# A new order inside the steps of layer 0: features first, the output product in the middle, routing last, the maxima unpromoted

## The chip, the cores and the metric

The kernel runs on one core of a Trainium2 chip. The metric is the device time of one execution in microseconds; three executions of the kernel before took 2866.75, 2875.81 and 2886.9 us, median 2875.81. The profile is of one further execution.

## The reference

A network of two layers works on 64 sequences of 128 rows and 128 features, with 77 context rows for each sequence. Each layer adds a gated attention to the context and then a gated mixture of 8 experts:

```
x = x + tanh(g_xattn[0]) * L0_attention(ctx, ctx, layernorm(x))
x = x + tanh(g_ffn[0])   * L0_experts(layernorm(x))
x = x + tanh(g_xattn[1]) * L1_attention(layernorm(x), ctx, ctx)
x = x + tanh(g_ffn[1])   * L1_experts(layernorm(x))
```

The change is in layer 0. Its attention has 16 heads. Queries, keys and values each go through the feature map `z = x @ fm_w.T + fm_b`, `[exp(z), exp(-z)]`, which makes 16 features of 8; scores are products of these over sqrt(128), softmax over the 77 context rows, a weighted sum of the value features, and an output product with `fc_w`. Its experts compute `silu(g) * u` on 336 inner features each and a down product; a router's softmax gives each expert's score, and a small second network picks for every row how many of the best experts count.

## The kernel before, in words

**Units and groups.** Layer 0's attention works on units of two sequences (32 units); the experts work on groups of four sequences (16 groups), so a group is two units. One unit passes through four generators, each in another step of the main loop in `run`:

- `l0_features` (step k for unit k): loads x and the context, layernorm on DVE and POOL, transposes into `pt`, the feature product `pz`, exponentials on ACT, transposes of the value features (`pv`), the split of the features into three bf16 parts (`split3`, DVE and POOL), the DMAs of these to DRAM (`dq`, `dk`) and back, stacked, into `qst` and `kst` (L331, L333).
- `l0_maxima` (step k+1): 32 products of `qst` and `kst` into the PSUM tile `S` (L346), six at a time, each group reduced to row maxima on DVE (L349); then the maxima are transposed (`pn`, L354), split in three on ACT, DVE and POOL (L357 to L360), and sent by three small DMAs into rows 96 to 98 of `qst` (L362).
- `l0_weighted` (step k+2): the transposed products, with the maxima subtracted inside the product (`ST`, L387), exponential on ACT (L390), the product with the value features (`AV`, L376), and at the end `od`, a DMA to DRAM, with `normalize`: DMAs, a reciprocal, and a POOL product that makes `o` (L437).
- `l0_project` (step k+3): the output product `pf` of `o` and `fc_w` (8 matmuls, L411) and the residual sum into `x1` (L413).

Every second step, from step 4 on, also holds `route` of the group whose second unit has just been projected: layernorm, transposes `ptf` (L449), the router's product `pr`, the small network, transposes into `pl` (L469, L470, L474), softmax and ranks on DVE, a split, and transposes `pp` (L590).

**The tape.** The experts' work is one long generator, cut into 33 parts a group. `tape(n)` plays n parts of it inside a step. A part is a hidden product (three matmuls each for `pg` and `pu`, L156 to L158, then ACT, DVE, DVE, ACT, POOL) or a down product (`py`), which begins with the expert's scores spread over a tile (`pb`, L599). `step` is given a target of `PARTS0 / 2 * (k + 1 - 5.0)` parts for step k, and plays as many as are missing.

**What sets the order.** `weave` interleaves a step's generators: each has a start and an end as shares of the step, its parts stand evenly between, and the parts are written into the program in the order of these positions. That is the program order. Each engine's list is planned from it before the run, on a modelled time line: of the instructions that are ready in the model, the one earliest in program order is taken. `high_priority(offset)`, the third number of an entry of `PLAN`, counts a part's instructions as if they stood that many places earlier. On the chip each engine works through its list in order and waits on semaphores where the data isn't there.

**Shared buffers.** Tiles of one tag take turns in program order. `pt`, `pz`, `pv`, `pn`, `pf`, `pl`, `pp` and `pb` all have the tag `misc` with one PSUM bank; `S`, `ST`, `AV` and `py` have one bank each; `pg`, `pu`, `ptf` and `pr` share three. `qst` has three buffers, `kst` three fixed tiles taken in turn.

**Queues.** SP issues all DMAs of layer 0, in one planned list.

After the last unit comes a transition: a step with the projection of unit 31, routing of group 15 and the first work of layer 1, planned with the same entries `out` and `rt0`; the later steps are layer 1's.

Of the kernel before, what the change touches and what calls it, by code (L numbers as in the profile page):

```python
# [41 lines left out]
def weave(tc, streams):  # L42


    todo = []
    for n, (gen, parts, lo, hi, pri) in enumerate(streams):
        todo.append([lo, n, gen, (hi - lo) / max(parts, 1), pri])
    while todo:
        t = min(todo, key=lambda x: (x[0], x[1]))
        try:  # L50
            if t[4]:
                with tc.high_priority(offset=t[4]):
                    next(t[2])
            else:
                next(t[2])
            t[0] += t[3]
        except StopIteration:
            todo.remove(t)


PARTS0, PARTS1 = 33, 24

PLAN = dict(
    out=(0, 0.2, 2000),
    wei=(0, 0.7, 0),
    max=(0.2, 0.95, 1000),
    fea=(0.2, 0.6, 1000),
    out1=(0.25, 0.4, 600),
    att1=(0.1, 0.95, 0),
    rel1=(0.37, 0.93, 0),  # L70
# [3 lines left out]
    t0=(0, 1.1, 0),  # L74
# [3 lines left out]
    prjT=(0, 0.55, 1000),  # L78
    attL=(0.1, 0.4, 500),
    prjL=(0.2, 0.3, 500),  # L80
    rt0=(0.1, 1, 500),
    rt1=(0.45, 0.7, 1000),
)

# [11 lines left out]
class Net:  # L96
# [947 lines left out]
    def run(self, ngroups):  # L1044
        tc, nc = self.tc, self.nc
        ctx = ExitStack()
        self.xs, self.routed = {}, {}
        self.done = 0
        self.ng = ngroups
        self.work = self.experts(ngroups)  # L1050

        self.fp = ctx.enter_context(tc.tile_pool(name="work", bufs=1))

        self.s3, self.ns3 = [], 0
        for n in range(2):
            t = self.fp.tile([128, GT], BF16, name=f"s3{n}", tag=f"s3{n}")
            nc.gpsimd.memset(t, 0.0)
            self.s3.append(t)
        ps = {n: ctx.enter_context(tc.tile_pool(name="ps" + n, bufs=1, space=PSUM)) for n in ("m", "S", "T", "A", "y")}
        self.pmisc, self.pS, self.pST, self.pY = ps["m"], ps["S"], ps["T"], ps["y"]  # L1060
        self.avp = ps["A"].tile([128, 4, 128], F32, tag="AV", name="AV")
        nc.vector.memset(self.avp, 0.0)
        gcm, self.pGU = self.pool("psg0", space=PSUM)
        self.gub = 3
        fcm, f0 = self.pool("f0")
        self.f0 = f0
        self.f0_open, self.ctx1 = (fcm, gcm), ctx
        acm, self.ap = self.pool("a0", side="right")
        self.l0_setup(f0, self.ap)
        nun = ngroups * 2  # L1070
        st = {}
        for k in range(nun + 2):
            w = []
            if 0 <= k - 3:
                w.append((self.l0_project(k - 3, st.pop(k - 3), self.xs), 1, *PLAN["out"]))
            if 0 <= k - 2 < nun:
                w.append((self.l0_weighted(st[k - 2]), 9, *PLAN["wei"]))
            if 0 <= k - 1 < nun:
                w.append((self.l0_maxima(st[k - 1]), 7, *PLAN["max"]))
            if k < nun:  # L1080
                w.append((self.l0_features(k, st), 5, *PLAN["fea"]))
            if k >= 4 and k % 2 == 0:
                w.append((self.route((k - 4) // 2), 6, *PLAN["rt0"]))
            self.step(w, 20, PLAN["t0"], math.ceil(PARTS0 / 2 * (k + 1 - 5.0)),
                      (k - 3) // 2 if k > 2 and k % 2 else None)
            if k == 1:
                with tc.issue_after(self.last_dma.ins):
                    self.l0_ffn_setup(f0)
        acm.__exit__(None, None, None)

        w1cm, w1 = self.pool("w1", side="right")
        self.l1_setup(w1)
        rpcm, self.rp = self.pool("rp", side="right")
        self.rqb, self.early = 2, 0
        acm, self.ap = self.pool("a1h", side="right")
        self.pp = self.ap
        self.l1_buffers(2)
        self.weights(2)
        self.banks = itertools.cycle(((self.pS, "S"), (self.pST, "ST")))
        s1 = {}  # L1100
        h0, h1 = (0, 0, 2), (0, 2, 2)
        self.step([(self.l0_project(nun - 1, st.pop(nun - 1), self.xs), 1, *PLAN["out"]),
                   (self.route(ngroups - 1), 6, *PLAN["rt0"]),
                   (self.l1_project(*h0, s1), 8, *PLAN["prjT"]),
                   (self.l1_relate(h0, s1), 7, *PLAN["relT"])], 27, PLAN["t0"])
        self.step([(self.l1_attend(s1[h0], 2), 13, *PLAN["attL"]),
                   (self.l1_project(*h1, s1), 8, *PLAN["prjL"]),
                   (self.l1_relate(h1, s1), 7, *PLAN["relL"])], self.parts(ngroups) - self.done, PLAN["t0"])
        while self.f0_open:
            next(self.work)  # L1110
        for k in range(1, ngroups + 3):
            w = []
            u = (k - 2, 0, 4) if k > 2 else h1 if k == 2 else h0
            if k == 2:
                weave(tc, [(self.l1_out(*u, s1.pop(u)), 3, 0, 1, 600), (self.tape(6), 6, 0, 1, 0)])
            elif k - 2 < ngroups:
                w.append((self.l1_out(*u, s1.pop(u)), 3, *PLAN["out1"]))
            if k == 2:

                acm.__exit__(None, None, None)  # L1120
                rpcm.__exit__(None, None, None)
                rpcm, self.rp = self.pool("rp4", side="right")
                self.rqb, self.early = 3, 2
                acm, self.ap = self.pool("a1", side="right")
                self.weights(4)
            if k == 1:
                w.append((self.l1_attend(s1[h1], 2), 13, *PLAN["attL"]))
            elif k - 1 < ngroups:
                w.append((self.l1_attend(s1[k - 1, 0, 4], 4), 23, *PLAN["att1" if k < ngroups else "attE"]))
            if k < ngroups:  # L1130
                w.append((self.l1_project(k, 0, 4, s1), 8, *PLAN["prj1"]))
                w.append((self.l1_relate((k, 0, 4), s1), 13, *PLAN["rel1"]))
            if 0 <= k - 2 < ngroups:
                w.append((self.route(ngroups + k - 2), 6, *PLAN["rt1"]))
            self.step(w, 28, PLAN["t1" if k < ngroups else "tE"],
                      self.parts(ngroups) + PARTS1 * (k + 1 - 3.0), ngroups + k - 2 if k > 2 and k - 2 < ngroups else None)
        for _ in self.tape(1000):
            pass
        for cm in (acm, rpcm, w1cm, self.ppcm):
            cm.__exit__(None, None, None)  # L1140
        ctx.close()
# [105 lines left out]
```

## Time and profile before

| | |
|---|---|
| median of three runs | 2875.81 us |
| profiled execution | 2871.89 us |
| its span, first to last instruction | 2870.2 us |
| mean granted TensorE clock | 0.921 |
| layer 0, first feature product to last projection | 6.1 to 1395.2 us |
| PE, DVE, ACT, POOL busy, 130 to 1330 us | 1053.29, 936.19, 674.30, 662.67 of 1200 us |
| PE busy, 0 to 130 us | 66.13 us |
| DMA queue of SP (q1), whole span | 246.28 MB, 42.8% of the time of 16 engines |

How to read it: busy time is per engine, PEld is the weight load that runs beside PE's matmuls, and PEclk is the clock granted to TensorE in tenths. A line of waits names the engine, the tile and line that waited, what came last before it could go on, the total in microseconds, how often, and the longest. In a timeline row stand the start, the duration, the engine, the line, the operation and its tiles (output, arrow, inputs), and in brackets the idle time of the engine before it with what ended it. Layer 0 is best read in its steady part, 130 to 1330 us; before that its pipeline fills, after it the two layers overlap.

### The profile page before, as it was taken

The numbers are of one execution on the slowest core, as the hardware profiler recorded it, in microseconds if no ns is written. First come the engines' busy times: TensorE is split into PE (matmuls) and PEld (weight loads), VectorE is DVE, ScalarE is ACT, GpSimd is POOL, SyncE is SP. The second block draws the span as 40 slices with busy tenths as digits, with TensorE's granted clock in tenths as the row PEclk, the third lists the DMA queues.
The fourth block names the chain that finished last, engine by engine and source line by source line (L and its number), as shares of the span: only waits on it lengthen the run. The fifth ranks groups of instructions, "written<-read, shape, count | busy, mean of one in ns | idle before, by whom it ended". The sixth has DMA issues, their size and how long they took to land.

```text
span 2870.2 us, 61032 instructions
## 1 busy us (share of the span) xinstructions
PE 2452.1 (85%) x23631; PEld 1668.7 (58%) x23638; DVE 1935.3 (67%) x4054; ACT 1579.2 (55%) x3030; POOL 1574.0 (55%) x1508
## 2 busy tenths in 40 slices
PE   3788898888888888988887878898988889889887
PEld 2455665666566565656554556566665666556654
DVE  3468787777878778777764555566566666656655
ACT  2455565555555555555543445566655556556556
POOL 4455555565545555455645535565555556555556
PEclk9989999999999999999986778899999999999998
DMA  6743534544445445343244655554554556555500
GB/s 144 163 103 96 106 91 83 116 98 95 97 84 105 107 93 101 87 85 77 77 84 108 137 104 119 116 110 108 109 115 104 118 119 126 116 105 113 108 16 8
DMA packets 504412, 290.56 MB, mean 101 GB/s; under 512 B 264614, under 2 KB 480814, under 8 KB 504027
## 3 DMA queue, kind: packets, MB, share of 16 engines
q1 hardware_dynamic: 476475, 246.28, 42.8%
q10 hardware_dynamic: 27648, 40.38, 4.0%
q8 instruction: 186, 3.05, 0.4%
q14 instruction: 103, 0.84, 0.1%
HBM read 147.19 MB, written 138.60 MB: 100 GB/s over the span
## 4 chain that ended last, share of the span: by engine, by line
PE 42%; DVE 19%; DMA 18%; POOL 8%; issue 7%; ACT 4%; SPq 3%; ACTq 0%; POOLq 0%; DVEq 0%
PE py L156 3%; PE ST L827 3%; PE py L157 3%; DMA qst<-dq 2%; DMA qst<-n 2%; PE py L158 2%; PE AV L376 2%; PE pz L156 2%; DVE t L508 2%; PE pg L156 2%; POOL hl L987 2%; PE S L770 2%; DVE t L509 2%; DMA kst<-dk 2%; PE ST L387 2%
## 5 line engine op out<-in xcount | busy, mean ns | idle before, releaser
L515 POOL TENSOR_TENSOR hl<-t,hh 128x512 fp32r<-128x512 f32 x336 | 454.0, 1357 | 345.3 <-ACT hh L514 339.0
L987 POOL TENSOR_TENSOR hl<-t,hh 128x512 fp32r<-128x512 f32 x256 | 345.2, 1362 | 111.6 <-ACT hh L986 111.1
L819 POOL TENSOR_TENSOR sc<-sc,mx 128x308 f32<-128x308 f32 x256 | 192.1, 752 | 216.0 <-DVE mx L818 139.5
L507 ACT ACTIVATE t<-pg 128x512 f32<-128x512 f32 x336 | 200.7, 598 | 160.6 <-PE pg L158 104.3
L514 ACT CAST hh<-t 128x512 fp32r<-128x512 f32 x336 | 207.8, 619 | 137.4 <-DVE t L509 58.0
L613 DVE TENSOR_TENSOR ys<-sb,py 128x512 f32<-128x512 f32 x224 | 153.2, 684 | 190.0 <-ACT sb L604 105.0
L828 ACT ACTIVATE rel<-ST 77x512 f32<-77x512 f32 x256 | 157.9, 617 | 187.3 <-PE ST L827 185.7
L508 DVE SCALAR_TENSOR_TENSOR t<-t,pg 128x512 f32<-128x512 f32 x336 | 226.8, 675 | 40.7 <-ACT t L507 40.2
L509 DVE TENSOR_TENSOR t<-t,pu 128x512 f32<-128x512 f32 x336 | 226.7, 675 | 10.8 <-PE pu L158 3.8
L604 ACT COPY sb<-pb 128x512 f32<-128x512 f32 x256 | 150.3, 587 | 134.7 <-PE pb L599 88.5
L817 DVE TENSOR_TENSOR sc<-S,rq 128x308 f32<-128x308 f32 x256 | 121.4, 475 | 147.8 <-PE ST L827 73.2
L986 ACT CAST hh<-t 128x512 fp32r<-128x512 f32 x256 | 158.5, 624 | 109.8 <-PE py L158 82.7
L614 POOL TENSOR_TENSOR acc<-acc,ys 128x512 f32<-128x512 f32 x96 | 133.6, 1391 | 154.5 <-DVE ys L613 154.2
L390 ACT ACTIVATE P<-ST 77x512 f32<-77x512 f32 x256 | 151.1, 591 | 120.3 <-PE ST L387 115.5
L979 ACT ACTIVATE t<-pz 128x512 f32<-128x512 f32 x256 | 153.3, 599 | 71.6 <-POOL hl L987 64.3
L827 PE MATMUL ST<-ident,sc 128*128 128x128 f32 (+1 forms) x1024 | 182.8, 307 | 5.1 <-ACT sg L776 1.6
L349 DVE TENSOR_REDUCE mx<-S 128x5 f32<-128x385 f32 (+1 forms) x192 | 110.3, 576 | 107.4 <-PE S L346 106.5
L156 PE MATMUL pu<-xh,wu_h 128*128 128x512 f32 x336 | 159.1, 473 | 21.9 <-DVE t L508 20.7
L156 PE MATMUL pg<-xh,wg_h 128*128 128x512 f32 x336 | 161.4, 480 | 15.7 <-DVE t L509 10.2
L157 PE MATMUL py<-hl,wd_h 128*128 128x512 f32 x336 | 150.9, 449 | 23.3 <-POOL hl L515 22.8
L156 PE MATMUL py<-hh,wd_h 128*128 128x512 f32 x336 | 152.0, 452 | 17.8 <-DVE ys L613 13.4
L827 PEld LDWEIGHTS ST<-ident,sc 128*128 128x128 f32 (+1 forms) x1024 | 131.7, 157 | 43.3 <-issue 14.2
(248 smaller groups left out, 6572.1 us busy)
## 6 DMA issues: line engine op xcount, KB each, us to landing
rq<-ra SPq DMA_DIRECT2D x256, 154.0 KB
qst<-dq SPq DMA_DIRECT2D x96, 384.0 KB
ra<-sg ACTq DMA_DIRECT2D x128, 192.5 KB
kst<-dk SPq DMA_DIRECT2D x96, 231.0 KB
dq<-f SPq DMA_DIRECT2D x47, 384.0 KB
od<-av SPq DMA_DIRECT2D x32, 512.0 KB
ra<-sg ACTq DMA_DIRECT2D x64, 231.0 KB
dq<-f SPq DMA_DIRECT2D x47, 256.0 KB
```

Source lines behind the costliest of these rows:

```text
L156: nc.tensor.matmul(ps, lhsT=wh, rhs=xh, start=start, stop=False)
L157: nc.tensor.matmul(ps, lhsT=wh, rhs=xl, start=False, stop=False)
L507: nc.scalar.activation(t, pg, AF.Tanh, scale=0.5)
L508: nc.vector.scalar_tensor_tensor(t, t, 1.0, pg, ALU.add, ALU.mult)
L509: nc.vector.tensor_tensor(t, t, pu, ALU.mult)
L514: nc.scalar.copy(hh, t)
L515: nc.gpsimd.tensor_tensor(hl, t, hh.bitcast(F32), ALU.subtract)
L819: nc.gpsimd.tensor_tensor(sc, sc, m.unsqueeze(2).to_broadcast([128, 4, KL]), ALU.subtract)
L827: nc.tensor.transpose(st[:r, j, :], sc.rearrange("q j k -> q (j k)")[:, j * KL : j * KL + r], self.ident)
L828: nc.scalar.activation(relg[:KL, hg, b], st[:KL].rearrange("k j (q e) -> k j q e", e=2), AF.Exp, scale=1.0 / math.sqrt(HD))
L986: nc.scalar.copy(hh, t)
L987: nc.gpsimd.tensor_tensor(hl, t, hh.bitcast(F32), ALU.subtract)
```

## The change

Only the positions, the promotions and one constant of layer 0's steps change:

- features: from 0.2 to 0.6 of a step to 0 to 0.4, still 1000 places ahead;
- the output product of the unit of three steps ago: from the start of the step (2000 places ahead) to 0.5 (1000 ahead);
- routing: from 0.1 to 1 to 0.55 to 1, still 500 ahead;
- the maxima: from 0.2 to 0.95 with 1000 places ahead to 0.1 to 0.85 with none;
- the weighted products: from 0 to 0.7 to 0.1 to 0.75, with no promotion before or after;
- the experts' target: 5.3 steps behind instead of 5.0;
- the transition's step gets entries of its own (`outT`, `rtT`) with the old values.

No instruction is added or taken out.

```diff
 PLAN = dict(
-    out=(0, 0.2, 2000),
-    wei=(0, 0.7, 0),
-    max=(0.2, 0.95, 1000),
-    fea=(0.2, 0.6, 1000),
+    out=(0.5, 0.55, 1000),
+    outT=(0, 0.2, 2000),
+    rtT=(0.1, 1, 500),
+    wei=(0.1, 0.75, 0),
+    max=(0.1, 0.85, 0),
+    fea=(0, 0.4, 1000),
...
-    rt0=(0.1, 1, 500),
+    rt0=(0.55, 1, 500),
...
-            self.step(w, 20, PLAN["t0"], math.ceil(PARTS0 / 2 * (k + 1 - 5.0)),
+            self.step(w, 20, PLAN["t0"], math.ceil(PARTS0 / 2 * (k + 1 - 5.3)),
...
-        self.step([(self.l0_project(nun - 1, st.pop(nun - 1), self.xs), 1, *PLAN["out"]),
-                   (self.route(ngroups - 1), 6, *PLAN["rt0"]),
+        self.step([(self.l0_project(nun - 1, st.pop(nun - 1), self.xs), 1, *PLAN["outT"]),
+                   (self.route(ngroups - 1), 6, *PLAN["rtT"]),
```

## The prediction

> **What bounds the kernel now.** I read the page first, then the windows by stage, then PE's waits in the longest stage of layer 0, then stretches of the timeline. The page names PE:
>
> ```profile
> PE 2452.1 (85%) x23631; PEld 1668.7 (58%) x23638; DVE 1935.3 (67%) x4054; ACT 1579.2 (55%) x3030; POOL 1574.0 (55%) x1508
> PEclk9989999999999999999986778899999999999998
> ```
>
> The change touches layer 0, so the stage that counts is its steady part, 130 to 1330 us. There PE works 1053.29 of 1200 us and DVE 936.19 (78%):
>
> ```profile
> 130.00:1330.00 1200.00, 1053.29 (x7111) 717.12 (x7104) 936.19 (x1829) 674.30 (x1317) 662.67 (x569) 0.95 0.45 97
> ```
>
> So 147 us of PE's time are idle, and this is what they waited for:
>
> ```profile
> PE S L346 <- DMA kst<-dk: 55.0, 24, 4.8
> PE pu L156 <- DVE t L508: 19.3, 31, 1.5
> PE py L157 <- POOL hl L515: 17.2, 15, 2.3
> PE py L156 <- DVE ys L613: 13.4, 11, 2.3
> ...
> PE ST L387 <- DMA qst<-n: 6.8, 14, 1.1
> PE S L346 <- DMA cg<-in_ctx_dram: 5.2, 1, 5.2
> ```
>
> The largest item is the maxima's first product (L346) standing at the head of PE's list while its stacked keys are still on their way: 55.0 us, and the 5.2 put down to cg is the same wait, one unit's. One case, on PE's timeline:
>
> ```profile
> 791.58 0.30 PE L297 MATMUL pt<-ident,cg 77*128 77x77 f32 x2
> 796.72 0.55 PE L346 MATMUL S<-kst,qst 96*128 96x77 bf16 x6 [4.85 <-DMA kst<-dk]
> 797.35 0.65 PE L387 MATMUL ST<-qst,kst 99*77 99x128 bf16 x4
> 797.75 0.77 PE L157 MATMUL py<-hl,wd_h 128*128 128x512 f32 x1
> 798.32 0.63 PE L158 MATMUL py<-hh,wd_l 128*128 128x512 f32 x1
> ```
>
> L387 and L157 come after L346 in PE's list and have to stand behind it. And after the wait the expert matmuls last 0.63 us where they lasted 0.39 to 0.40 before it: the granted clock of 792 to 799 is 0.65. In the clock records 22 stretches of 3.4 or 6.8 us at half clock lie in the stage (122.9 us), and 13 of them (71.7 us) begin within 4.5 us of the start of one of these waits.
>
> The other thing to see is what keeps the steps in order. All of pt, pz, pv, pn, pf, pl, pp, pb share one PSUM bank, and the timeline shows them taking it in program order, whatever their priority:
>
> ```profile
> 700.75 1.61 PE L411 MATMUL pf<-fcw,o 128*128 128x128 f32 x8
> 704.30 0.38 PE L295 MATMUL pt<-ident,ln_xn 128*128 128x128 f32 x2
> 723.68 0.22 PE L469 MATMUL pl<-ident,lgT 8*128 8x8 f32 x1
> 738.13 0.28 PE L354 MATMUL pn<-ident,mx 128*32 128x128 f32 x1
> 757.62 0.39 PE L590 MATMUL pp<-identb,p3b 128*24 128x128 bf16 x4
> 762.84 1.05 PE L411 MATMUL pf<-fcw,o 128*128 128x128 f32 x8
> 785.85 0.27 PE L354 MATMUL pn<-ident,mx 128*32 128x128 f32 x1
> 788.32 1.10 PE L411 MATMUL pf<-fcw,o 128*128 128x128 f32 x8
> ```
>
> This is a step with routing (pf at 700.75 to pf at 762.84, 62 us) and one without (25.5 us), 87.6 us a pair; the stage holds 13.6 pairs.
>
> **What the change leaves alone.** It adds and removes no instruction and no DMA. All of it is order, so every term is a wait that goes, comes or moves.
>
> **Maxima without priority, features first.** Today a unit's maxima, 1000 places ahead, go onto PE the moment the planner believes the keys landed; on the chip they land later, and PE stands. By unit, the 14 waits of odd units (whose features stand in steps without routing) sum to 45.6 us, the others to 14.6. Unpromoted, the maxima take their place among expert matmuls that are ready. Does the data then come first? Unit 19: pt at 767.23, keys in use at 796.72, so 29.5 us from pt to landing. An even unit's pt will be first in its step and its maxima a tenth into the next; even with the shorter step of the two (25.5 us) and the 27 us of softmax that precede the next step's pt, that is over 40 us: **its waits go, -14.6 us**. An odd unit's pt can't start before pp (757.62), which the bank's order puts before it; its keys land some 30 us after pp, and the step in which its maxima stand begins 22 to 25 us after pp plus a tenth of a 44 us step, 27 to 30 us. That is a draw. Bounds 0 and -45.6; I take half, **-22.8**, for it lies on the boundary.
>
> **The clock.** The 71.7 us at half clock cost at most 35.9 of work; at 792 about 2.6 of a 6.8 us stretch was spent waiting anyway, so about two thirds, 24 us, can come back. The short waits of even units seldom trigger it; half of 24, **-12** (0 to -36).
>
> The Trainium skill ("TensorE: Matmul & The Clock Gate", Part 1, the HAM clock gate) says that the clock halves after an idle window of about 3.4 us. The trace is stricter with this kernel: a wait of 2.05 us at 693.06 us was followed by 6.8 us at half clock. By the rule only the seven odd-unit waits above 3.2 us would count, at 3.4 us each, and the term would be at most -24; by the rows it is -12 as taken.
>
> **The output product in the middle.** pf (8 matmuls, 1.1 to 1.6 us) waits for o. The last weighted product of unit 16 ended at 731.7, o at 753.6, 22 us later, and pf came at 762.84: 9 us to spare, given by the bank, not by the data. Afterwards the weighted products end three quarters into a step and pf stands half into the next: 0.75 x 43.8 = 33 us against 22. But pf keeps a promotion of 1000, so where o is late PE stands as it did for the keys. Today that is 1.5 us in the whole stage; the worst single row is 2.2 us (87.1 us), and 27 units of that would be 59. I take a sixth, **+10** (0 to +59): nearer the 1.5, as 11 us are spare. What queues behind it: pn, pl and the next pb on the bank, the expert matmuls on PE.
>
> **The row of maxima (qst<-n).** pn moves from 0.84 of the step to 0.74, but unpromoted, and the weighted products from 0 to 0.1 of the next: 0.36 x 43.8 = 16 us instead of 0.16 x 43.8 = 7. The n DMAs take 6.5 us from pn to L387 (738.13 to 744.6). In the steps without routing pn follows the expert scores, so it can slip: **+7** (from -7, all of today's, to +23, 1.1 us for each of 27 units).
>
> **SP.** Per unit some 21 DMAs keep their number; od waits longest at the head of SP (215.7 us in 26 waits, up to 16.6). The keys' DMAs move ahead in the step, od moves from 0.7 to 0.75. I count 0, for SP's list is written in the same planned time as PE's. The skill ("DMA: Bandwidth & Descriptors", Anatomy of one DMA) speaks against that: a DMA's semaphore wait is held by the issuing sequencer before dispatch, so a key DMA planned behind an od that is late on the chip is late too; by it the odd units' -22.8 would become 0.
>
> **Routing, 5.3 for 5.0.** Routing moves to 0.55 of the step and the expert work falls back by 0.3 x 16.5 = 5 parts. By my count of parts ptf and pr then stand behind the same experts as today (parts 21 and 22 of 33), but pp stands before the score of the expert at part 27 where today it stands before part 30. From 730.5 (the last of pl) to 757.62 DVE works through the softmax between expert instructions, and that 27 us is covered by what PE can run ahead: it is busy 24.1 of 28 us there. One expert less is 18 matmuls of 0.236 us, 4.2 us, that move behind pp; the weighted products of the odd unit (some 8.5 us), ready earlier, take their place. I count **0**.
>
> **Start and end.** At the start pt of unit 3 waits for pf of unit 0 (89.3 us, pt at 93.1) though unit 2's pz came at 43.4; features first lets it start some 20 us earlier, and pp of the first group, 148.0, about 10 earlier: **-8** (0 to -15). The 5 parts (189 matmuls x 0.236 / 33 = 1.35 us each, 6.8 us) move into the transition, where outT and rtT keep the old order: 0 (+-7). The expert chain's own waits (pu, pg, py: 66 us) I leave: 0 (-10 to +15), for a denser PE gives their engines less time.
>
> **Sum:** -14.6 - 22.8 - 12 - 8 + 10 + 7 = -40.4 us. The profiled execution took 2871.89 us (span 2870.2), 3.9 under the median of the three runs: **2831.5 us**, 1.4% less.
>
> **Rivals.**
> *The bank becomes the bound (slower).* Place: routing's end, pp, on the shared bank. For: pp now precedes an earlier expert, and the next step's features queue behind it. If the odd weighted products don't fill in, 4.2 us of cover go per pair, and the 6.3 us from pt to the last pv (767.23 to 773.5) stand bare as well: 4.2 to 10.5, say 8 x 13.6 = +109, less the 57 above: 2924 us. It decides above 57 / 13.6 = 4.2 us a pair. Against: PE's idle time inside the softmax is under 4 us of 28.
> *The waits move.* Odd units wait as now, and even units' 14.6 come back as waits for n and o: 2872 - 8 - 5 = about 2859.
> *It doesn't act.* The bank's order, not priority, set the maxima's place, and keys still land last: only the start changes, about 2864.
>
> **Chances:** forecast 0.56, bank-bound 0.22, moved 0.12, no effect 0.10. The last two are within 1% (28.7 us, about what a measurement of this kernel can tell from no change). Range: down to all key waits and 24 us of clock gone with 15 of the start, -99, rounded to 2768; up to near the slower rival, 2918. Left out: about 0.05 below, 0.13 above.
>
> **What would show it.** Right: L346 <- kst under 30 us in the stage, the stage's clock up from 0.95, pairs of 84 to 85 us. Wrong: new PE waits at L411 for o or L387 for n; PE idle between pl and pp; pairs over 88 us with pt waiting for pp. What would make me wrong most is the planner's order, which I infer from positions: a single DMA that it believes early on a promoted instruction costs 27 waits.

## The result: 4.4% slower, and the profile after

The changed kernel takes 3002.09 us (median of six runs, 2989.49 to 3014.57) against 2873.64 for the kernel before in the same session: a ratio of 1.0441, 95% interval 1.0405 to 1.0477. The forecast was 2831.5 with a range up to 2918, so the sign was wrong, and the time is 84 us above the upper end of the range. The profiled execution has a span of 2994.2 us, 124.0 more than before. In the code of the changed kernel, and in all lines below but that of experiment 6, line numbers are two higher than before (L346 is now L348).

The page's busy times and its clock row:

```profile
PE 2514.0 (84%) x23630; PEld 1700.5 (57%) x23638; DVE 1896.3 (63%) x4054; ACT 1579.1 (53%) x3030; POOL 1547.0 (52%) x1508
PEclk9989888988999899988999688999999999999998
```

The work is the same, yet PE is busy 62 us longer: the clock row has many more eights in its first half, which is layer 0. DVE, ACT and POOL have not become busier; none of them became the bound. The windows by stage say the same of the steady part. Columns are the window, its length, the busy time of PE, PEld, DVE, ACT and POOL with their instructions, the granted clock, the DMA share and GB/s; the upper row is the kernel before, the lower the changed one:

```profile
420.00:1300.00 880.00, 772.74 (x5202) 527.06 (x5201) 689.36 (x1337) 497.69 (x971) 487.55 (x418) 0.95 0.45 97
```

```profile
420.00:1300.00 880.00, 743.28 (x4705) 500.06 (x4703) 599.43 (x1211) 449.24 (x880) 423.84 (x379) 0.90 0.39 89
```

In the same 880 us PE gets through 4705 matmuls where it got through 5202, at a clock of 0.90 for 0.95. Every engine and the DMA queues do less at the same time, so something that all of them follow has become longer.

**It is not the waits that I counted.** PE's waits in the steady part (130 to 1430 us, which in this kernel holds 13.4 pairs of steps; total, count, longest):

```profile
PE S L348 <- DMA kst<-dk: 36.5, 17, 3.9
PE ptf L451 <- DVE ln_xn L121: 30.4, 13, 3.6
PE pu L158 <- DVE t L510: 20.5, 24, 3.4
PE pg L158 <- DVE t L511: 20.1, 28, 1.5
PE pp L592 <- POOL p3b L131: 13.3, 11, 3.3
```

The wait for the stacked keys, 55.0 + 5.2 us in 13.6 pairs before, is down to 36.5 by this name. Five more waits of 2.3 to 3.5 us stand in the same place, in front of a unit's first maxima, and the profile puts them down to `qst<-n` (6.8), to `qst<-dq` (2.3) or to nothing that it sees (6.0). With these it is 51.6 us, and by the pair the fall is from 4.4 to 3.9. New is a wait of the router's transposes `ptf` for the layernorm of the rows that `pf` has just completed, once in every pair.

**It is the turn on the shared bank.** Of the timeline, the first row of each tile with the tag `misc` that matters, and `ptf`, over one pair of steps; all other rows are left out:

```profile
687.59 0.63 PE L297 MATMUL pt<-ident,ln_xn 128*128 128x128 f32 x2
...
694.58 0.85 PE L304 MATMUL pz<-xT,fmW 128*128 128x410 f32 x2
...
701.80 0.38 PE L320 MATMUL pv<-ident,feat 128*77 128x128 f32 x2
...
703.42 1.16 PE L413 MATMUL pf<-fcw,o 128*128 128x128 f32 x8
...
706.73 0.28 PE L356 MATMUL pn<-ident,mx 128*32 128x128 f32 x1
...
710.59 0.47 PE L451 MATMUL ptf<-ident,ln_xn 128*128 128x128 f32 x1 [2.98 <-DVE ln_xn L121]
...
724.64 0.22 PE L471 MATMUL pl<-ident,lgT 8*128 8x8 f32 x1
...
749.76 0.39 PE L592 MATMUL pp<-identb,p3b 128*24 128x128 bf16 x4 [0.91 <-POOL p3b L131]
...
751.86 0.44 PE L297 MATMUL pt<-ident,ln_xn 128*128 128x128 f32 x2 [0.68 <-ACT sb L606]
...
768.42 1.05 PE L413 MATMUL pf<-fcw,o 128*128 128x128 f32 x8
...
772.19 0.27 PE L356 MATMUL pn<-ident,mx 128*32 128x128 f32 x1
...
786.95 0.63 PE L297 MATMUL pt<-ident,ln_xn 128*128 128x128 f32 x2
...
803.40 1.16 PE L413 MATMUL pf<-fcw,o 128*128 128x128 f32 x8
```

Read it as one loop. In the step with routing, the features come first (`pt` at 687.59, `pz`, the last `pv` at 701.80) and only then may `pf` have the bank, at 703.42: 15.8 us after `pt`. Routing needs the rows that `pf` completes, so `ptf`, `pl` and the softmax follow from there, and `pp` comes at 749.76. The next features `pt` stand behind `pp` on the same bank (751.86, 2.1 us later), then `pf` and `pn` of the step without routing, and then the next even unit's `pt` at 786.95. Before, `pf` was first in its step: its row stood at 700.75 and `pt` behind it at 704.30, so the features' passage through the bank lay beside routing.

One leg of this loop is not the bank's: the one from `pf` at 768.42 to `pt` at 786.95. Its rows are those of the input `x`:

```profile
769.51 0.48 DVE L415 SCALAR_TENSOR_TENSOR x<-pf,tgates,xg 128x256 f32<-128x256 f32 x1 [0.83 <-PE pf L413]
...
770.09 0.40 SPq L289 DMA_DIRECT2D xg<-in_x_dram  x1
...
777.79 1.43 DVE L121 TENSOR_SCALAR ln_xn<-xg,ln_mv,ln_rs 128x128 f32<-128x128 f32 x2
```

`xg` has four buffers, so a unit's load waits until the unit four places earlier has had its residual sum (L415), which comes right behind `pf`. The load was issued 0.1 us after that sum, and the layernorm ended at 779.22. The bank, too, was free by 779.32, when its last tile, a `pb`, had been read. PE came to `pt` 7.6 us later, after a wait of 3.86 us for keys and the matmuls that stand before it in PE's list. Over the ten pairs `pt` of the even units starts 5.8 us after its layernorm; before the change it was 20.9 us. So the loop goes through the bank at `pp` to `pt` and at `pt` to `pf`, and through the buffer of `x` and PE's list on the way back.

The starts of these tiles on PE, averaged over ten pairs of the steady part of each profile (the fourth to the thirteenth group), put numbers on the loop; a negative value means that `pf` came before `pt`:

| us per pair | before | after |
|---|---|---|
| `pp` to the next even unit's `pt` | 36.0 | 36.7 |
| that `pt` to `pf` in the same step, which routing waits for | -3.8 | 15.5 |
| `pf` to `pp` (router, softmax, ranks) | 55.6 | 45.1 |
| one pair | 87.8 | 97.0 |
| PE idle | 10.7 | 15.0 |
| at half clock | 8.5 | 20.1 |

(The parts are averaged over slightly other pairs than the whole, so they add to 97.3 in the last column.) `pf` falls 19.3 us later behind `pt`; routing, with a more compact place, gains 10.5 back; with 0.7 from `pp` to `pt` that is 9.5, and by the pairs themselves 9.2 us a pair. From the first `pp` to the fourteenth, thirteen pairs, the profiles show 1138.1 us before and 1255.7 after, +117.6. The first `pp` is 21.4 later (169.4 for 148.0), and from the fourteenth `pp` to the end 15.0 come back. The sum is the 124.0 of the spans.

PE's time gives the same figure from its side: 4.3 us more idle, and 11.6 us more at half clock. By estimate about half of that, 5.8, is work stretched, for at half clock the expert matmuls start every 0.43 us instead of every 0.23 (784.81 and 777.15 us in the changed kernel). That makes 10.1 a pair against 9.2.

### The profile page after: what moved, and what is told of

Its sections match the earlier page's. It is cut to its first block, busy times and chain, and to the rows that moved or that the text cites. A ratio compares the mean times of both kernels' runs of the same rounds, so it can differ in the third digit from the quotient of the medians.

```text
span 2994.2 us, 61112 instructions
## 1 busy us (share of the span) xinstructions
PE 2514.0 (84%) x23630; PEld 1700.5 (57%) x23638; DVE 1896.3 (63%) x4054; ACT 1579.1 (53%) x3030; POOL 1547.0 (52%) x1508
## 4 chain that ended last, share of the span: by engine, by line
PE 47%; DMA 20%; DVE 15%; POOL 6%; ACT 4%; SPq 4%; issue 4%; ACTq 0%; POOLq 0%; DVEq 0%
PE py L158 4%; PE ST L829 3%; PE py L159 3%; DMA kst<-dk 3%; PE py L160 3%; DMA qst<-dq 2%; PE pu L158 2%; PE pz L158 2%; PE pg L158 2%; PE AV L378 2%; PE S L772 2%; PE AV L837 2%; DMA qst<-n 2%; PE S L877 2%; PE ST L389 2%
## 5 line engine op out<-in xcount | busy, mean ns | idle before, releaser
L517 POOL TENSOR_TENSOR hl<-t,hh 128x512 fp32r<-128x512 f32 x336 | 438.6, 1313 | 442.3 <-ACT hh L516 434.8
L989 POOL TENSOR_TENSOR hl<-t,hh 128x512 fp32r<-128x512 f32 x256 | 345.5, 1364 | 113.2 <-ACT hh L988 112.6
L616 POOL TENSOR_TENSOR acc<-acc,ys 128x512 f32<-128x512 f32 x96 | 125.8, 1310 | 125.5 <-DVE ys L615 121.7
L158 PE MATMUL pg<-xh,wg_h 128*128 128x512 f32 x336 | 169.9, 506 | 22.1 <-DVE t L511 21.6
L158 PE MATMUL pu<-xh,wu_h 128*128 128x512 f32 x336 | 166.2, 495 | 22.4 <-DVE t L510 22.0
L158 PE MATMUL py<-hh,wd_h 128*128 128x512 f32 x336 | 159.1, 474 | 11.5 <-DVE x L581 6.2
L348 PE MATMUL S<-kst,qst 96*128 96x77 bf16 x1024 | 77.1, 213 | 95.1 <-DMA kst<-dk 68.3
L158 PE MATMUL pz<-xh,w1s_h 128*128 128x512 f32 x256 | 130.4, 510 | 27.9 <-ACT t L981 27.7
```

The lines of the kernel that those rows point to most:

```text
L158: nc.tensor.matmul(ps, lhsT=wh, rhs=xh, start=start, stop=False)
L517: nc.gpsimd.tensor_tensor(hl, t, hh.bitcast(F32), ALU.subtract)
L989: nc.gpsimd.tensor_tensor(hl, t, hh.bitcast(F32), ALU.subtract)
```

## The experiments

The theory: the loop `pp`, `pt`, `pf`, `pp` through the one bank has become the bound, because `pf` now stands behind the features. The rivals that were tried: the 5.3 puts an expert's score into that loop; the maxima without promotion lose more than their waits; the new PE waits (`ptf`) and the half clock are the cause and not the sign. A fourth, that the later `pf` frees the buffers of `x` too late, was not tried by a fifth buffer; experiment 7 speaks to it. All kernels compute the whole reference.

### 1. The output product first again

```diff
-    out=(0.5, 0.55, 1000),
+    out=(0, 0.2, 2000),
```

> The changed kernel with the output product back at the start of the step, 2000 places ahead; the rest as changed. Bank theory: the 15.5 us that pf of an odd unit stands behind the step's features (pt to pf) leave the pair's cycle; the pair falls from 97.0 us to 86 to 92, the time to 2860 to 2930. Theory that the unpromoted maxima are to blame: the pair stays at 95 us or more, 2980 to 3010.

Measured: 1.0014 of the kernel before (0.9995 to 1.0032). The pair is back at 87.8 us, `pt` to `pf` at -6.0, half clock at 7.5 us a pair. The one entry of `PLAN` carries the whole loss. With it the waits for the keys are back too (63.1 us in 27 waits, 4.3 us a pair), though the maxima are still unpromoted and the features still nominally first: on the bank they stand behind `pf` again.

### 2. The maxima promoted again, at their old place

```diff
-    max=(0.1, 0.85, 0),
+    max=(0.2, 0.95, 1000),
```

> The changed kernel with the maxima's old entry (0.2 to 0.95, 1000 ahead). Bank theory: the cycle is unchanged, and the waits for the keys come back from 2.1 to about 4.5 us a pair: 2990 to 3040. Theory of the unpromoted maxima: falls under 2930.

Measured: 1.0398 (1.0376 to 1.0421); the pair 96.2, `pt` to `pf` 15.7. The loss stays: the new entry of the maxima is not what costs. The waits in front of a unit's first maxima are 59.1 us by all their names (4.4 a pair), but 33.2 by the name `kst<-dk`, so the expected 4.5 came by the first count alone.

### 3. The experts' target at 5.0 again

```diff
-math.ceil(PARTS0 / 2 * (k + 1 - 5.3))
+math.ceil(PARTS0 / 2 * (k + 1 - 5.0))
```

> The changed kernel with the experts at 5.0 steps behind again. Bank theory: five parts of the experts move against the bank's other users, pp stands behind a score more, but features still stand before pf: within 1% of the changed kernel, 2970 to 3030. Theory that the later experts are to blame: under 2930.

Measured: 1.0418 (1.0387 to 1.045); the pair 97.5. The loop is distributed in another way (`pp` to `pt` 25.9, `pt` to `pf` 20.5, `pf` to `pp` 50.5) and is as long. The 5.3 is not the cause of the loss.

### 4 and 5. The output product on another bank, in both kernels

```diff
-        pf = pm.tile([128, 512], F32, tag="misc", name="pf")
+        pf = self.pGU.tile([128, 512], F32, tag="gu", bufs=self.gub, name="pf")
```

> The changed kernel with pf in the three banks of the hidden products (tag gu) instead of the shared bank; every position stays. Bank theory: pf no longer waits for pt, pz and pv; pt to pf falls from 15.5 us to under 8, the pair to 86 to 92, the time to 2850 to 2930. If the pair is long because of new stalls at ptf and pp and the half clock behind them (20.1 us of it a pair, 8.5 before), it stays above 2970.

> The kernel before with pf in the three banks of the hidden products: the control of the same edit in the changed kernel. Bank theory: pf stands before the features there, so it waits for nothing of them; little to win, pair 86 to 89 us, within 1% of before. If the edit by itself makes any version faster (a bank less contended), it gains 2% or more, and the recovery of the changed kernel by it proves less.

Measured: with this edit the changed kernel takes 1.0026 (1.0005 to 1.0048) of the kernel before, and the kernel before takes 1.0149 (1.0122 to 1.0176). So the edit in itself costs 1.5%, more than the 1% expected, with a pair of 90.8 us; `pf` then takes turns with the hidden products, but whether that is the reason was not followed up. And yet it removes all but 0.3% of the loss from the changed kernel, whose order is otherwise left as it was. `pf` still starts 12.1 us after `pt`, but it no longer holds `pn`, `pl` and `pp` nor is held by `pz` and `pv`; the pair is 89.1 us, half clock 8.9.

The Trainium skill ("Perfetto Trace Analysis", Optimizing Tensor Performance, Matmuls) says that independent groups of matmuls should take different PSUM banks in turn, so that the emptying of one lies beside the next. The two runs agree with it for the changed order and disagree for the old one (1.0149): another bank helped where the turn on the bank is in the loop, and cost where it is not.

### 6. The maxima unpromoted, alone, in the kernel before

```diff
-    max=(0.2, 0.95, 1000),
+    max=(0.1, 0.85, 0),
```

> The kernel before with the maxima alone unpromoted and at 0.1 to 0.85. My prediction's step (promotion puts them on PE before their keys): waits for the keys fall from 4.5 us a pair to 2 or less, 1 to 2% faster than before. Rival, from the kernel with the output product first, where they stayed at 4.3 us: the keys are what comes last at either priority, waits 4 us or more, within 0.7% of before.

Measured: 1.0094 (1.006 to 1.0129), a loss. PE's wait for the keys, by its waits from 130 to 1330 us:

```profile
PE S L346 <- DMA kst<-dk: 63.0, 23, 5.2
```

They are as long as before the change (55.0 and the 5.2 put down to `cg`). Without promotion, and 0.1 of a step earlier, the maxima reach PE's head before the keys all the same. This edit does not tell the promotion from the place; experiments 7 and 13 (below), which differ in the promotion alone, do: 37.3 and 34.4 us of waits by this name. The promotion was not the cause of those waits.

### 7 and 8. The routing's last product on another bank, in both kernels

```diff
-        s["sd"] = self.scores_out(p)
+        s["sd"] = self.scores_out(p, self.pS, "S")
...
-    def scores_out(self, p):
+    def scores_out(self, p, pool=None, tag="misc"):
...
-        pp = self.pmisc.tile([128, 1024], BF16, tag="misc", name="pp")
+        pp = (pool or self.pmisc).tile([128, 1024], BF16, tag=tag, name="pp")
```

> The changed kernel with pp in the maxima's bank (tag S) instead of the shared one, nothing else. Bank theory: the next step's features no longer queue behind routing's softmax; the loop features, pf, routing, pp, features is open, the pair falls from 97 to 84 to 90 us, 0 to 3% off the kernel before on either side. If pt to pf in the same step (15.5 us) is enough to make it long by itself, it stays above 93 us, over 2% slower than before.

> The kernel before with pp in the maxima's bank. If its pair of 87.8 us is also set by the shared bank's loop (pf to pp 55.6, pp to pf 32.2), the loop opens here too: 83 to 86 us, 1.5 to 3% faster than before. If PE's work with its waits sets it, 87 to 89 us and within 1%.

Measured: the changed kernel with it 0.9966 (0.9952 to 0.998), the kernel before with it 1.013 (1.0112 to 1.0148). In the changed kernel this opens the loop at its other end: the next `pt` no longer stands behind `pp`, and the pair is 87.0 us although `pt` to `pf` is still 12.8. It also tells the sign from the cause. PE's waits of the changed kernel with this edit:

```profile
PE S L348 <- DMA kst<-dk: 37.3, 12, 4.3
PE ptf L451 <- DVE ln_xn L121: 32.4, 13, 2.9
```

The wait of `ptf` is as long as in the changed kernel (30.4) while the loss is gone, so that wait is not the loss. Nor is the buffer of `x` by itself: the layernorm of the even units still ends 10.3 us after their load was issued (10.2 in the changed kernel), `pt` starts 8.6 us after it (5.8), and nothing is lost. Half clock falls from 20.1 to 11.9 us a pair with nothing done to it but the loop: the larger part of the half clock followed the loop.

The kernel before misses both of its expectations with this edit: the pair is 91.5 us, not 83 to 89. There `o` is ready only 1.6 us before `pf` of the odd units starts, where it was 9.7, so another wait has come forward; it was not followed up.

### 9. The kernel before with features ahead of the output product

```diff
-    out=(0, 0.2, 2000),
+    out=(0.19, 0.2, 2000),
+    outT=(0, 0.2, 2000),
+    rtT=(0.1, 1, 500),
-    fea=(0.2, 0.6, 1000),
+    fea=(0, 0.4, 1000),
-    rt0=(0.1, 1, 500),
+    rt0=(0.25, 1, 500),
```

> The kernel before with one thing of the change: features at 0 to 0.4, the output product at 0.19 (2000 ahead, as before) and routing from 0.25, so that pt, pz and pv stand ahead of pf on the shared bank; maxima promoted, experts at 5.0, weighted products and the transition as before. Bank theory: pf starts 10 to 16 us after pt where it started 3.8 us before it; the pair grows to 93 to 98 us, 3 to 5% slower than before. If the loop needs the late routing or the unpromoted maxima too, it stays within 1.5% of before.

(The transition has its old values through `outT` and `rtT`, as in the changed kernel.) Measured: 1.025 (1.0216 to 1.0284). Here nothing is changed but the order of features and output product, and routing after them. It lies between the two expectations. On the timeline, the rows of the loop's tiles:

```profile
715.39 0.34 PE L592 MATMUL pp<-identb,p3b 128*24 128x128 bf16 x3
...
720.29 0.38 PE L297 MATMUL pt<-ident,ln_xn 128*128 128x128 f32 x2
...
752.84 0.63 PE L297 MATMUL pt<-ident,ln_xn 128*128 128x128 f32 x2
...
763.73 1.13 PE L413 MATMUL pf<-fcw,o 128*128 128x128 f32 x8
```

In the step with routing (the last two rows) `pf` again stands behind `pt`, 10.9 us here and 10.2 on the average, and the pair is 93.5 us. The swap alone is thus enough for 2.5% of the 4.4%; some of it, 2.0 us of the 5.7 a pair, is met by longer waits for the keys (6.56 us a pair for 4.57), so it is not the bank's turn alone.

### 10 and 11. Both cures, and routing unpromoted

Experiment 7 with the maxima promoted at their old place (as in 2), and then with `rt0=(0.55, 1, 0)` too:

```diff
-    max=(0.1, 0.85, 0),
+    max=(0.2, 0.95, 1000),
...
-    rt0=(0.55, 1, 500),
+    rt0=(0.55, 1, 0),
```

> The changed kernel with pp in the maxima's bank and the maxima promoted as before. The unpromoted maxima alone cost the kernel before 0.9%, 10 us of it before the first pp: with them promoted again 0.3 to 0.8% under the kernel with pp moved alone, 0.989 to 0.994 of before. If promotion does nothing once the bank's loop is open: 0.995 to 0.998 of before. One loss is possible: the maxima's bank is then asked for early and pp waits in it, up to 1.005.

> As the kernel with pp moved and the maxima promoted, with routing's promotion of 500 taken away. Theory that the stall at ptf (2.4 to 2.6 us a pair, half clock behind it) comes from planning ptf the moment the model believes the layernorm done: the stall goes under 0.5 us a pair, up to 2.5 us a pair faster, 0.3 to 1%. Bank theory adds: routing gets longer without promotion, and where it holds pl longer the loop closes again: slower by 1% or more.

Measured: 1.0373 (1.0344 to 1.0401) and 1.0375 (1.0349 to 1.0401). The second edit does nothing, to the wait of `ptf` neither (16.4 and 17.0 us). The first brings the loss back that moving `pp` had taken away, which I had not expected.

### 12. The experts' target at 5.15

```diff
-math.ceil(PARTS0 / 2 * (k + 1 - 5.3))
+math.ceil(PARTS0 / 2 * (k + 1 - 5.15))
```

> The changed kernel with the experts 5.15 steps behind instead of 5.3. By the parts this takes the one expert score that stands between pt and pz off that place on the shared bank (in steps with routing pf then follows pt, pz, pv, pv at once), and the next score stands behind pf. Bank theory: pt to pf falls from 15.5 us to 9 to 12, the pair from 97.0 to 91 to 95, 1.5 to 3.5% slower than before instead of 4.4. If the expert score between them is not what makes 15.5 of 10.2 (the kernel before with pf and features swapped), pt to pf stays over 14 and the time over 4% above before.

Measured: 1.0366 (1.0306 to 1.0426); the pair 94.5 and `pt` to `pf` 14.1. It was to take the expert's score (`pb`) out from between `pt` and `pz`, where the changed kernel has it in all ten pairs, and it did: in all ten the bank's turns are now `pt`, `pz`, `pv`, `pv`, `pf`, and the next score stands behind `pf`. The rows of these tiles in one pair:

```profile
767.88 0.64 PE L297 MATMUL pt<-ident,ln_xn 128*128 128x128 f32 x2
...
771.26 0.92 PE L304 MATMUL pz<-xT,fmW 128*128 128x410 f32 x2
...
780.05 0.38 PE L320 MATMUL pv<-ident,feat 128*77 128x128 f32 x2
...
782.97 1.05 PE L413 MATMUL pf<-fcw,o 128*128 128x128 f32 x8
...
786.32 0.39 PE L601 MATMUL pb<-s,sel 128*128 128x512 bf16 x1
```

With that `pt` to `pf` shrank by 1.4 us, not by the 3.5 to 6.5 expected. So the score is not what makes 15.5 here of the 10.2 in experiment 9. The time is 0.8% lower, but the interval overlaps the changed kernel's.

### 13. Maxima promoted, but at their new place

Experiment 7 with the promotion alone:

```diff
-    max=(0.1, 0.85, 0),
+    max=(0.1, 0.85, 1000),
```

> The changed kernel with pp in the maxima's bank and the maxima promoted by 1000 at their new place, 0.1 to 0.85. Between the kernel with pp moved alone (87.0 us a pair, 0.9966 of before) and the one with the maxima's whole old entry (95.9, 1.037). If the promotion takes the gain of the moved pp: 94 us or more, 1.03 to 1.04. If the place does (pn behind pl on the shared bank): 86 to 88 us, 0.99 to 1.00.

Measured: 0.9942 (0.9922 to 0.9961) of the kernel before, the fastest of all: 0.6% better than before, and it differs from experiment 10 only in the place of the maxima, 0.1 to 0.85 of the step for 0.2 to 0.95. The two timelines, rows of the bank's users, first experiment 10 and then experiment 13:

```profile
729.01 0.34 PE L592 MATMUL pp<-identb,p3b 128*24 128x128 bf16 x3
...
756.96 0.27 PE L356 MATMUL pn<-ident,mx 128*32 128x128 f32 x1
...
762.19 0.41 PE L297 MATMUL pt<-ident,ln_xn 128*128 128x128 f32 x2
...
776.82 1.16 PE L413 MATMUL pf<-fcw,o 128*128 128x128 f32 x8
```

```profile
756.20 0.39 PE L592 MATMUL pp<-identb,p3b 128*24 128x128 bf16 x4
...
773.97 0.27 PE L356 MATMUL pn<-ident,mx 128*32 128x128 f32 x1
...
784.44 0.44 PE L297 MATMUL pt<-ident,ln_xn 128*128 128x128 f32 x2
```

In experiment 10 the row of maxima `pn` comes 28.0 us after `pp`, and the even unit's `pt` 5.2 us behind it. The layernorm of that `pt` had ended at 755.27, so `pt` stood for the turn on the bank, behind `pn` and two `pb`. In experiment 13 `pn` comes 17.8 us after `pp`. So `pn` is a second tile that can hold the bank, with `pp` off it. It is not the whole difference: over ten pairs `pp` to that `pt` is 34.1 us in experiment 10 and 29.5 in 13, `pt` to `pf` 15.7 and 12.4, and a pair 95.9 and 86.3. And `pn` of the step with routing differs as well: in 10 it comes behind `pl`, 38.8 us after its maxima were ready, in 13 ahead of `pl`, 8.3 us after. The place of the maxima, 0.1 of a step, makes the loss here; which of these turns carries it is not shown, as `pn` had no bank of its own in any run.

## Why the prediction was wrong

**The step that failed is the output product in the middle, with "Routing ... I count 0".** I asked there whether the data, `o`, comes before `pf`, and priced the wait of PE if not (+10). The data was never late: PE waited once at L413, 0.7 us, and that not for `o`, and `pf` now comes 54 to 66 us after its unit's last product with the value features where it came 22 to 28 us after. I did name what queues behind `pf` (`pn`, `pl`, the next `pb`), but gave it no price, and I had written that its 9 us to spare were "given by the bank, not by the data". I left out that the same bank then keeps `pf` behind `pz` and `pv`, and that routing starts from `pf`. The features of the step with routing (`pt` to the last `pv`, 13 to 16 us) went from beside routing into the line ahead of it: `pt` to `pf` is 15.5 us where it was -3.8, and a pair 97.0 where it was 87.8. Experiments 1, 4 and 7 open the line in three ways and lose 0.3% or less; 9 makes it in the kernel before. Of the signs that I had set, the last one came: pairs over 88 us with `pt` behind `pp`.

**The rival "The bank becomes the bound" named the place, and not the turn that costs.** It had the shared bank and the next features behind `pp`, but priced PE standing bare there, not `pf` behind the features. It said 8 us a pair gross, less 57 us of gains: 2924 us. Measured are 9.2 net, of which 4.3 are PE idle. Two of its terms were off. Its bare stretch of 6.3 us was read from an odd unit (767.23 to 773.5), whose features run alone; the line leads through the even unit's, and `pt` to `pf` there is 15.5 us. And of the gains it subtracted 8.6 us came.

**The gains, term by term.**

- *Key waits, -14.6 and -22.8.* In front of a unit's first maxima, whatever the profile names, they fell from 60.2 to 51.6 us: the odd units' from 45.6 to 33.1, and the even units', which I had called gone, rose from 14.6 to 18.6. With the loop open, in experiments 7 and 13, the even units' are gone (0.7 us) and the odd units' are 41.0 and 37.7. The cause that I gave, promotion, was wrong (experiments 6, 7 and 13), and earlier features alone do not do it (93.2 us in experiment 9). In experiments 10 and 11 PE does not wait for keys at all in the steady part, and yet it idles 13.6 us a pair in both, and a pair is 95.9 and 96.5 us: where the loop sets the pair, a wait less on PE becomes another wait on PE.
- *Clock, -12.* The other way: half clock in layer 0 rose from 133.1 to 293.5 us.
- *Start, -8.* +21.4. `pt` of unit 3 did come earlier (64.5 for 93.1), but the first `ptf` was later (127.2 for 110.1) and the first `pp` with it. Of this, 15.0 came back from the fourteenth `pp` on; that it is the 0.3 steps by which the experts lag, moved into the transition, is likely and wasn't tried.
- *Row of maxima, +7.* The wait at L389 fell to 3.9 us in the whole stage from 6.8 before. Two waits of 6.8 us together bear the name `qst<-n` at L348, but stand in front of the first maxima of units 23 and 29, and are counted with the keys above.
- *SP, 0.* The odd units' key waits are neither whole nor gone, so the runs don't tell whether something on SP holds them. No run shows a part of the loss in it.
- *5.3 for 5.0, 0.* Held in size: 1.0418 with 5.0.

Two slips bear on none of this: 731.7 is the end of unit 16's last `ST`, and its last `AV` ended at 736.7; and 99 us under 2871.89 is 2773, not 2768.

**What stays open.** The swap in the kernel before gives 2.5%, the whole change 4.4%. The maxima's new setting costs 0.9% in the kernel before (experiment 6) but nothing in the changed one (experiment 2, with the old setting, is 0.4% lower, within the intervals); an expert's score within the loop adds some 0.8 by the medians, within the intervals too (experiment 12). What makes 15.5 us of `pt` to `pf` where the swap alone makes 10.2, and how the rest joins to 1.9%, is not settled. What the leg through the buffer of `x` adds was not tried alone. The kernels with a tile on another bank differ by the price of that edit, too, 1.3 and 1.5% in the kernel before.

## What to carry to other kernels

Where short-lived tiles share a buffer and take turns in program order, as here, priority lifts no step past its turn: write down the order of the turns and follow the loop through it before counting any engine's waits; the loop can also leave the buffer, as it does here through the buffers of `x`. Of a step that is moved, ask what waits for it as well as what it waits for; "time to spare" on the way in says nothing of the way out. And an engine that is 88% busy with a table of waits is not yet the bound: if the waits go and the period stays long, as in experiment 10, it was a follower.

## What the hardware showed beside this

Half clock more than doubled (8.5 to 20.1 us a pair) while PE's busy share of the steady part changed little (772.74 and 743.28 of 880 us), so the share alone does not set it. After the 2.98 us wait of `ptf` at 710.59, shown above, the windows of the changed kernel give the clock before and after it:

```profile
700.00:707.00 7.00, 7.00 (x81) 4.97 (x79) 4.45 (x11) 3.79 (x8) 4.24 (x4) 1.00 0.07 21
711.00:718.00 7.00, 5.67 (x18) 3.97 (x17) 3.59 (x8) 2.29 (x4) 1.36 (x2) 0.50 0.72 187
```

The clock records show 13.7 us at half speed from 709.9 on, though PE had been fully busy 3 us earlier and worked 5.67 of the 7 us that follow. The Trainium skill ("TensorE: Matmul & The Clock Gate", Part 1, the HAM clock gate) says that the clock halves after an idle window of about 3.4 us; here a wait shorter than that was enough. But the kernel of experiment 7 has the same waits of `ptf`, up to 2.9 us, with 11.9 us of half clock a pair: the wait alone does not decide, and what does was not tried.
